# Layer 1 of a two-layer graph network: the turned weights with the key tile innermost, 128 queries in one set of TensorE weights

## The chip, the core and the metric

The kernel runs on one core of a Trainium2 chip. The time is device microseconds of that core for one execution of the whole program; lower is better. TensorE multiplies matrices (PE in the profile, and PEld for its loads of weights), VectorE (DVE), ScalarE (ACT) and GpSimd (POOL) do the rest, and SyncE (SP) starts most of the DMA transfers. Engines run side by side and wait for each other through semaphores; each one works through its own instructions in order.

## What is computed

There are 16 graphs of 1024 nodes with 256 features, and an integer matrix `adj` for each graph. Layer 0 is attention with 8 heads of 32, masked by `adj`. Layer 1 is a graph attention without projections. Cut to what matters here:

```
h = relu(layernorm(x));  x = x + attention_0(h, adj)         # 8 heads, mask adj == 0
h = relu(layernorm(x))
e_k    = leaky_relu(einsum('bid,bjd->bij', h * a_k, h), 0.2)   # k = 0..3
scores = where(adj == k + 1, e_k, -9e15)                       # one of the four, by adj
alpha  = softmax(scores)
x      = x + einsum('bij,bjd->bid', alpha, h)                  # the sums of this change
```

`adj` holds only 0 and 1 in these inputs, so layer 1 uses `a_0` alone. A general path, `layer_1_of_kinds`, stands behind a condition and is not run.

## The kernel before, in words

**Tiles.** A graph is cut into 8 tiles of 128 query nodes (NT = 8), so there are 128 tiles in all. The main loop goes over the tiles s of all graphs, and within a tile over the 8 heads h of layer 0. The order of the work on each engine is written out by hand in this loop (under `tc.manual_schedule()`); nothing moves it. Layer 1 of a tile (class `Edges`) runs 9 tiles behind layer 0 (class `Attend`), and the projections of a tile (class `Piece`) run 9 tiles ahead, all of them spread over the heads of the tile that is in work. So 120 tiles of layer 1 lie inside the main loop; the last ones follow it in a loop of their own, the tail, which lays layer 1 of the remaining tiles behind each other (`last` is true for eight of them; they use other buffers and do the leaky ReLU on VectorE).

**Layer 0 in a tile.** For each head TensorE forms the scores (L461) in one of two PSUM buffers, `sides` (heads 4 and 6 in side 1, the others in side 0, but for the first tiles). VectorE adds the mask and takes the maximum (L473), and in reading the scores it also sets the buffer free. ACT takes the exponential (L490). Then the 128x1024 matrix has to be turned, so that the keys lie on the partitions. Some heads are turned on TensorE (`turn_half`, L590, with the copy L591 on ACT or VectorE), some by blocks: VectorE transposes 32x32 blocks (`blocks_of`, L381), and four DMA transfers put the blocks into their partitions (`placed`, L386). Which heads go by which way depends on the tile: 0, 1, 4 and 5 by blocks, but only 4 and 5 in the first tile of a graph and only 0 and 1 in the last. The keys stand in another order for the heads that usually go by blocks, so where such a head is turned on TensorE its exponential writes in a changed order (L482 to L488): heads 0 and 1 in the first tile of a graph, 4 and 5 in the last. The sums over the values follow (`combine`, L526): four heads of 32 columns beside each other in four column groups of TensorE's array, group 0 at head 7, group 1 at head 3 of the next tile.

**Layer 1 in a tile.** The edge matrix is symmetric, so half of its scores are transposed copies of blocks that are kept in `mirror` (L627), the others are matmuls (L633, at heads 0 and 2). VectorE masks (L656, head 3), ACT and GpSimd bend (L665, L674 to L676), ACT takes the exponential (L680, head 6). This leaves `sel`, 128 queries x 1024 keys. In the next tile:

- head 0: `turn_blocks` (L688) transposes `sel` by 32x32 blocks on VectorE, through the same line L381 as for the heads. `place_blocks` (L691) issues the four transfers into `pT1`.
- heads 5 and 6: `gather` (L694) forms the sums, in two halves of four key tiles each. The weights are the turned matrix, the moved operand is `h1s`, 128 keys x 256 features. The output has 128 queries, in four column groups of 32: for each key tile j and each group a one matmul with 32 columns of weights (L698).
- head 6: `store` divides by the softmax's total and adds the nodes (L705, L707) and writes out (L708).

The layout of the turned matrix before is `[block row b][key tile j][query q]` in each partition, with 8 key tiles of 32 queries each: the 32 queries of one block are contiguous. `placed` moves chunks of 1 KB, 256 elements, and after it one partition holds four groups a of `[j][q]`.

Rows of a tile are loaded in a mixed order and written back in it (`mixed`), so that the order of the queries in the turned matrix is that of the partitions of the sums.

Around the change, the order at the start of a tile is on VectorE: L473 of head 0, the turning of `sel` (L381), L473 of head 1. On TensorE: scores of head 0 (L461), transposes (L590), edge scores, scores of head 1, transposes, L565, projections (L267), scores of head 2.

Of the kernel before, what the change touches and what calls it, by code (L numbers as in the profile page):

```python
# [8 lines left out]
F32 = mybir.dt.float32  # L9
# [8 lines left out]
P = 128  # L18
HEADS = 8
HD = 32  # L20
# [27 lines left out]
def gnn_kernel(  # L48
# [18 lines left out]
    nc = tc.nc  # L67
    B, N, D = x.shape
    NT = N // P
# [3 lines left out]
    NB = P // HD  # L73
# [10 lines left out]
    work = ctx.enter_context(tc.tile_pool(name="work", bufs=2))  # L84
# [294 lines left out]
    def blocks_of(p):  # L379
        blocks = work.tile([P, NB, NT, HD], F32, tag="blocks", bufs=3)  # L380
        nc.vector.transpose(blocks.rearrange("p b j q -> p j b q"), p)  # L381
        return blocks.rearrange("p b j q -> p b (j q)")

    def placed(blocks, pT):
        for a in range(NB):
            nc.sync.dma_start(  # L386
                out=pT[:, a * NT * HD : (a + 1) * NT * HD], in_=blocks[a * HD : (a + 1) * HD]
            )
        return pT.rearrange("p (a j q) -> p j a q", a=NB, j=NT)


    h1s, x1ds, masks = {}, {}, {}
# [22 lines left out]
    class Attend:  # L415
# [82 lines left out]
        def turn_blocks(self, h):  # L498
            self.blocks = blocks_of(self.probs[h][0])

        def place_blocks(self, h):
            self.turned[h] = placed(self.blocks, ptp.tile([P, N], F32, tag="pT", name="pT"))
# [91 lines left out]
    class Edges:  # L594
# [91 lines left out]
            nc.gpsimd.dma_start(out=self.x1, in_=x1ds[self.b][self.rows, :])  # L686

        def turn_blocks(self):  # L688
            self.blocks = blocks_of(self.sel)

        def place_blocks(self):  # L691
            self.pT = placed(self.blocks, self.buffer("pT1", [P, N]))

        def gather(self, half):  # L694

            for j in range(half * NT // 2, (half + 1) * NT // 2):
                for a in range(NB):
                    nc.tensor.matmul(  # L698
                        self.sums[a * HD : (a + 1) * HD, :], lhsT=self.pT[:, j, a], rhs=h1s[self.b][:, j, :],
                        start=(j == 0), stop=(j == NT - 1),  # L700
                    )

        def store(self):
            rec = small.tile([P, 1], F32, tag="rec1")
# [82 lines left out]
    with tc.manual_schedule():  # L787
# [51 lines left out]
        for s in range(B * NT + 1):  # L839
            b, t = divmod(s, NT)  # L840
# [224 lines left out]
```

## Time and profile before

| | us |
|---|---|
| median of 3 runs | 3076.24 |
| lowest and highest | 3071.88, 3076.31 |
| the profiled execution, its own time | 3076.4 |
| its span, first to last instruction | 3074.5 |
| busy: ACT | 2654.5 (86%) |
| busy: GpSimd | 2177.6 (71%) |
| mean granted TensorE clock | 0.996 |

The groups of the profile that belong to the changed steps or lie next to them:

| group | count | busy us | mean ns |
|---|---|---|---|
| L526, sums of layer 0, four column groups | 16384 | 533.4 | 275 |
| L381, turning of `sel` | 120 | 148.8 | 1240 |
| L541, projection of the output, 128 columns of weights, 256 moved | 512 | 131.8 | 380 |
| L707, division and sum | 124 | 60.0 | 484 |

A row of the groups gives line, engine, operation, output and inputs by the names of the program, the shape and the number of instructions; behind the bar the busy time of all of them in us and the mean time of one in ns; then the idle time of the engine just ahead of them and what ended it. On TensorE an fp32 matmul leaves two records, and records overlap: a mean of 380 ns does not say that the next one has to wait so long. Busy is the time that the records cover together.

A row of the order in time gives the start in us from the span's first instruction, the time from the first start to the last end of a run of like instructions, the engine, the line, the names and the shape, the count, and in brackets the idle time ahead of it with what ended it.

### The profile page before, as it was taken

Reading aid. Unit: us, or ns where it says so; the run is one execution under the profiler, and the core shown is the slowest. Engines: PE = TensorE matmul, PEld = TensorE weight load, DVE = VectorE, ACT = ScalarE, POOL = GpSimd, SP = SyncE. Lnnn points to the kernel's source line nnn. Section 1 sums busy time; section 2 is a strip of 40 time slices with the busy share of each in tenths; the row PEclk is TensorE's granted clock in tenths of the full one; section 3 lists DMA queues with packets and bytes.
Section 4 is the critical chain, followed back from the end, with each engine's and each line's share of the span. In section 5 each row is a group of like instructions: output and inputs, shape, how many; then the busy total and the mean of one; then the engine's idle time right before and its main releaser. Section 6 shows DMA issues by size and latency. Waiting matters only on the chain. (4 is left out here: it accounts for less than half of the span.)

```text
span 3074.5 us, 96254 instructions
## 1 busy us (share of the span) xinstructions
PE 2965.6 (96%) x36722; PEld 2230.1 (73%) x36722; DVE 2515.6 (82%) x4453; ACT 2654.5 (86%) x5159; POOL 2177.6 (71%) x2999
## 2 busy tenths in 40 slices
PE   7889999999999999999999999999999999999998
PEld 5667777777777777777777777777777777776664
DVE  5878888888888888888888788888888888888885
ACT  5888888899898998889889888988989888898882
POOL 3657777777777777777777777777777777776542
PEclk9999999999999999999999999999999999999999
DMA  7766777877777786777777777787777777777653
GB/s 245 219 219 205 237 235 222 255 216 243 231 225 243 230 257 209 232 247 220 246 230 228 235 232 243 221 255 221 220 247 228 251 211 235 237 227 236 191 168 100
DMA packets 597828, 695.68 MB, mean 226 GB/s; under 512 B 63280, under 2 KB 528560, under 8 KB 597360
## 3 DMA queue, kind: packets, MB, share of 16 engines
q1 hardware_dynamic: 528288, 477.29, 51.9%
q0 software_dynamic: 66960, 210.04, 21.0%
q8 instruction: 295, 4.83, 0.7%
q10 hardware_dynamic: 2112, 2.10, 0.2%
q14 instruction: 173, 1.42, 0.1%
HBM read 252.98 MB, written 134.22 MB: 126 GB/s over the span
## 5 line engine op out<-in xcount | busy, mean ns | idle before, releaser
L473 DVE CUSTOM_DVE_ANT_0 p<-s,neg 128x1024 f32<-128x1024 f32 x1024 | 1236.2, 1208 | 220.7 <-PE s L461 185.1
L490 ACT ACTIVATE p<-p,nmx 128x1024 f32<-128x1024 f32 x1024 | 1249.4, 1224 | 132.5 <-DVE nmx L473 123.9
L461 PE MATMUL s<-k,qt 128*128 128x512 f32 x2048 | 760.6, 453 | 15.5 <-DVE nmx L473 4.3
L591 ACT COPY pT<-trp 128x512 f32<-128x512 f32 x1024 | 549.4, 590 | 95.3 <-PE trp L590 94.9
L590 PE MATMUL trp<-ident,p 128*128 128x128 f32 x4608 | 604.5, 274 | 4.7 <-ACT pT L591 1.5
L590 PEld LDWEIGHTS trp<-ident,p 128*128 128x128 f32 x4608 | 531.0, 140 | 104.0 <-ACT pT L591 10.8
L381 DVE STREAM_TRANSPOSE blocks<-p 128x1024 f32<-128x1024 f32 x456 | 564.5, 1238 | 12.3 <-ACT p L680 10.6
L526 PE MATMUL acc<-pT,v 128*32 128x128 f32 x16384 | 533.4, 275 | 41.8 <-ACT recT L520 30.0
L526 PEld LDWEIGHTS acc<-pT,v 128*32 128x32 f32 x16384 | 453.5, 110 | 153.0 <-ACT recT L520 85.0
L698 PE MATMUL acc<-h,pT 128*32 128x256 f32 x8192 | 496.9, 382 | 2.8 <-DVE h L707 1.7
L441 POOL TENSOR_SCALAR neg<-adj 128x1024 bf16<-128x1024 int32 x128 | 467.9, 3655 | 42.9 <-ACT neg L453 33.7
L461 PEld LDWEIGHTS s<-k,qt 128*128 128x128 f32 x2048 | 322.9, 191 | 106.3 <-issue 43.0
L698 PEld LDWEIGHTS acc<-h,pT 128*32 128x32 f32 x8192 | 241.8, 109 | 207.8 <-issue 65.6
L676 POOL TENSOR_TENSOR sel<-sel,less 128x1024 f32<-128x1024 f32 x120 | 286.8, 2390 | 68.9 <-ACT less L665 47.6
L633 PE MATMUL s<-h1T,ha 128*128 128x512 f32 (+2 forms) x744 | 272.8, 490 | 2.7 <-ACT h1T L569 1.6
L674 POOL TENSOR_SCALAR less<-top 128x1 f32<-128x1 f32 x120 | 31.9, 266 | 274.0 <-DVE top L656 273.9
L324 POOL DMA_DIRECT2D qd<-halves x240 | 177.5, 780 | 58.7 <-POOL halves L314 31.8
L490 ACT ACTIVATION_READ_ACCUMULATOR p<-p,nmx 128x1 f32 x1024 | 206.8, 202 | 0.0
L510 POOL COPY wide<-rec 128x256 f32<-128x256 f32 x128 | 53.8, 420 | 204.2 <-DVE rec L508 204.2
L330 POOL DMA_DIRECT2D kd<-halves x240 | 172.2, 766 | 35.5 <-POOL halves L314 35.4
L314 POOL TENSOR_TENSOR halves<-full,halves 128x256 fp32r<-128x256 f32 x240 | 176.8, 737 | 20.6
L633 PEld LDWEIGHTS s<-h1T,ha 128*128 128x128 f32 x744 | 126.7, 190 | 70.7 <-issue 45.0
(117 smaller groups left out, 4328.4 us busy)
## 6 DMA issues: line engine op xcount, KB each, us to landing
pT<-blocks SPq DMA_DIRECT2D x2304, 128.0 KB, 3.5
qt<-qd SPq DMA_DIRECT2D x128, 512.0 KB, 4.5
k<-kd SPq DMA_DIRECT2D x128, 512.0 KB, 7.3
adj<-in_adj POOLq DMA_DIRECT2D x127, 512.0 KB, 5.0
qd<-halves POOLq DMA_DIRECT2D x240, 256.0 KB, 2.7
kd<-halves POOLq DMA_DIRECT2D x240, 128.0 KB, 4.1
xb<-in_x POOLq DMA_DIRECT2D x128, 128.0 KB, 4.2
x1d<-x SPq DMA_DIRECT2D x128, 128.0 KB, 4.0
```

The lines of the kernel that those rows point to most:

```text
L324: nc.gpsimd.dma_start(out=qds[self.b][self.first, oc].rearrange("p u w n -> p u (w n)"), in_=halves.unsqueeze(1).to_broadcast([P, 2, 2 * P]),)
L381: nc.vector.transpose(blocks.rearrange("p b j q -> p j b q"), p)
L441: nc.gpsimd.tensor_scalar(self.neg, self.adj, 0.0, MASKED, ALU.is_equal, ALU.mult)
L461: nc.tensor.matmul(self.ps[:, cols], lhsT=self.qt[:, h, :], rhs=keysets[self.b][h][:, cols], start=True, stop=True,)
L473: nc.vector.tensor_tensor_reduce(out=p, in0=sides[h in self.second], in1=self.neg, scale=-SCALE, scalar=FLOOR, op0=ALU.add, op1=ALU.min, a ...
L490: nc.scalar.activation(to, of, AF.Exp, bias=nmx, scale=-1.0, accum_out=self.sums[:, h : h + 1])
L526: nc.tensor.matmul(sums_place[r * HD : (r + 1) * HD, g * P : (g + 1) * P], lhsT=vs[self.b][:, j, place_of(h) : place_of(h) + HD], rhs=self ...
L590: nc.tensor.transpose(tr[:, j, :], p[:, jj * P : (jj + 1) * P], ident)
L591: copy(pT[:, half * 4 : half * 4 + 4, :], tr)
L633: nc.tensor.matmul(self.side[:, cols], lhsT=self.ha[:, c, :], rhs=h1T[:, c, cols], start=(c == 0), stop=(c == NC - 1),)
L676: nc.gpsimd.tensor_tensor(self.sel, self.sel, self.less, ALU.subtract)
L698: nc.tensor.matmul(self.sums[a * HD : (a + 1) * HD, :], lhsT=self.pT[:, j, a], rhs=h1s[self.b][:, j, :], start=(j == 0), stop=(j == NT - 1),)
```

## The change

The edge matrix is no longer turned by the common helper `blocks_of`. `turn_blocks` of `Edges` has its own transpose, which writes each 32x32 block so that the key tile j is innermost: the layout becomes `[block row b][query q][key tile j]`. Neighbouring queries are then 8 elements (32 bytes) apart in a partition; before they were neighbours. The input is read as before.

The four transfers of `placed` are the same: 256 contiguous elements for each group, whatever order they have. After them a partition holds `[a][q][j]`, and since a and q are next to each other, the 128 queries of all four groups for one key tile are one row of elements at a stride of 8. `gather` takes them as one set of 128 columns of weights: for each key tile one matmul with an output of 128 partitions, in place of four with 32. In a tile that is 8 matmuls for 32. The moved operand, the number of key tiles, the place in PSUM (`sums`) and the halves stay. The order of all other instructions on each engine stays too, and the turning of layer 0's heads still goes through `blocks_of`.

```diff
         def turn_blocks(self):
-            self.blocks = blocks_of(self.sel)
+            blocks = work.tile([P, NB, HD, NT], F32, tag="blocks", bufs=3)
+            nc.vector.transpose(blocks.rearrange("p b q j -> p j b q"), self.sel)
+            self.blocks = blocks.rearrange("p b q j -> p b (q j)")
 
         def place_blocks(self):
-            self.pT = placed(self.blocks, self.buffer("pT1", [P, N]))
+            pT = self.buffer("pT1", [P, N])
+            placed(self.blocks, pT)
+            self.pT = pT.rearrange("p (aq j) -> p j aq", j=NT)
 
         def gather(self, half):
 
             for j in range(half * NT // 2, (half + 1) * NT // 2):
-                for a in range(NB):
-                    nc.tensor.matmul(
-                        self.sums[a * HD : (a + 1) * HD, :], lhsT=self.pT[:, j, a], rhs=h1s[self.b][:, j, :],
-                        start=(j == 0), stop=(j == NT - 1),
-                    )
+                nc.tensor.matmul(
+                    self.sums, lhsT=self.pT[:, j], rhs=h1s[self.b][:, j, :],
+                    start=(j == 0), stop=(j == NT - 1),
+                )
```

## The prediction

> **What bounds the kernel now.** I read the shares of the engines first, then the groups by line, then the instructions in order of time of one tile out of the middle (tile 5 of a graph, 1618 to 1633 us), because a mean over 3 ms does not say which wait ends last.
>
> ```profile
> PE 2965.6 (96%) x36722; PEld 2230.1 (73%) x36722; DVE 2515.6 (82%) x4453; ACT 2654.5 (86%) x5159; POOL 2177.6 (71%) x2999
> ...
> L381 DVE STREAM_TRANSPOSE blocks<-p 128x1024 f32<-128x1024 f32 x456 | 564.5, 1238 | 12.3 <-ACT p L680 10.6
> ...
> L698 PE MATMUL acc<-h,pT 128*32 128x256 f32 x8192 | 496.9, 382 | 2.8 <-DVE h L707 1.7
> ```
>
> TensorE is busy 96% of the span, no other engine over 86%. L698, the sums that change, takes 496.9 us: 64 records a tile (each fp32 matmul leaves two). Now the order on TensorE (columns: start, time to the last end, count):
>
> ```profile
> 1618.99 1.04 PE L590 MATMUL trp<-ident,p 128*128 128x128 f32 x8
> 1619.95 1.93 PE L698 MATMUL acc<-h,pT 128*32 128x256 f32 x32
> 1621.82 0.44 PE L237 MATMUL acc<-ident,h 128*128 128x128 f32 x2
> 1622.01 0.71 PE L461 MATMUL s<-k,qt 128*128 128x512 f32 x2
> 1622.65 1.93 PE L698 MATMUL acc<-h,pT 128*32 128x256 f32 x32
> 1624.52 1.16 PE L267 MATMUL acc<-hT,wkT 128*128 128x128 f32 x8
> 1625.43 0.70 PE L461 MATMUL s<-k,qt 128*128 128x512 f32 x2
> ...
> 1630.10 0.73 PE L461 MATMUL s<-k,qt 128*128 128x512 f32 x2
> 1630.66 1.03 PE L590 MATMUL trp<-ident,p 128*128 128x128 f32 x8
> 1631.54 0.38 PE L565 MATMUL acc<-ident,h 128*128 128x128 f32 x2
> 1631.75 1.06 PE L267 MATMUL acc<-hTm,wqT 128*128 128x128 f32 x8
> 1632.57 0.71 PE L461 MATMUL s<-k,qt 128*128 128x512 f32 x2
> ```
>
> Here the start-to-start times are to be read: one group follows the other without a hole, so a group costs what lies between its start and the next. And VectorE in the same stretch:
>
> ```profile
> 1628.81 1.23 DVE L473 CUSTOM_DVE_ANT_0 p<-s,neg 128x1024 f32<-128x1024 f32 x1 [0.18 <-POOL shift L172]
> 1629.96 0.08 DVE L473 DVE_READ_ACCUMULATOR2_ANT nmx<- 128x1 f32 x1
> 1629.96 1.24 DVE L381 STREAM_TRANSPOSE blocks<-sel 128x1024 f32<-128x1024 f32 x1
> 1631.12 1.19 DVE L473 CUSTOM_DVE_ANT_0 p<-s,neg 128x1024 f32<-128x1024 f32 x1
> 1632.24 0.08 DVE L473 DVE_READ_ACCUMULATOR2_ANT nmx<- 128x1 f32 x1
> ```
>
> Heads 0 to 3 share one scores buffer (side 0), so the scores of head 2 (TensorE, 1632.57) cannot start before VectorE's L473 of head 1 has read it (ends 1632.32). That L473 stands right behind the turning of the edge matrix (1629.96), which the change touches. TensorE starts 0.06 us after VectorE's end where it does wait (1630.04 to 1630.10, head 1), so at head 2 the slack is 0.25 - 0.06 = 0.19 us. The kernel is bound by TensorE, but at heads 0 to 2 VectorE is only 0.2 us from the path.
>
> **The change, part by part.**
>
> *The sums.* 32 matmuls a tile of 32 columns of weights become 8 of 128 columns: 64 records become 16, in two halves of 8 records. Four column groups run side by side, so a half takes 1621.82 - 1619.95 = 1.87 us, the second too (1624.52 - 1622.65). The eight full-width records of L267 with 128 columns moved take 1632.57 - 1631.75 = 0.82 us and the eight transposes 0.88, so about 0.107 us for 128 columns moved and 0.215 us for 256: a half will take 8 x 0.215 = 1.72 us. That saves 0.15 us a half, 0.30 a tile. Going over between full width and column groups costs too: eight transposes take 0.96 us ahead of L698 and 0.88 ahead of L565 (0.08); the scores 0.64 ahead of L698 and 0.56 ahead of L590 (0.08); L267 takes 0.91 behind L698 and 0.82 otherwise (0.09). Together **0.55 us a tile** that TensorE no longer needs.
>
> *The weights, now at a stride of 8 elements.* No row shows TensorE loading weights at a stride. 8 loads of 128 columns follow each other in the 0.82 us of L267, 0.10 us each, beside matmuls that are as short. From now on they lie beside matmuls of 0.215 us. A price of up to double is hidden; whatever is over it falls on TensorE 16 times a tile. Lower bound nothing. The nearest row of a strided access in SBUF is an ACT write:
>
> ```profile
> 1514.23 2.18 ACT L490 ACTIVATE p<-p,nmx 128x1024 f32<-128x1024 f32 x1
> ...
> 1517.47 2.22 ACT L490 ACTIVATE p<-p,nmx 128x1024 f32<-128x1024 f32 x1
> ...
> 1519.51 1.16 ACT L490 ACTIVATE p<-p,nmx 128x1024 f32<-128x1024 f32 x1
> ```
>
> These are the exponentials of heads 0, 1 and 2 of a first tile. By L482 to L488 heads 0 and 1 there write at a stride of 4 elements (16 bytes) and the others in order: 2.20 us against 1.15, 1.05 us more for 1024 elements, 1.03 ns each. For 128 columns that is 0.13 us on top of 0.107, 0.24 us against the matmul's 0.215: 0.025 x 16 = 0.4 us a tile. I take nothing, because a price that merely doubles is covered, and keep 0.4 for the range.
>
> *The turning on VectorE.* The 32x32 transpose now writes its elements 32 bytes apart, 128 times. Reading PSUM at a stride is free here (L242 692 ns at a stride against L591 684 ns in order), which is the lower bound, nothing; but this is a write into SBUF, and there the nearest row is the exponential above. By its 1.05 us more, 1.24 becomes 2.29; doubling the part that grows with the elements (1.24 less 0.16, the time of the 128x1 reciprocal L705) gives **1.08 us more**; by the ratio 2.20/1.15 it is 1.13. No row shows an access that a stride makes cheaper. I take 1.08.
>
> The Trainium skill (SBUF — State Buffer, section "SBUF: two separate sides") says that SBUF has lines of 16 bytes, that each access to a new line pays, and that fp32 can be strided by 4 for free. The exponentials are at exactly 4 and pay, so the measurement decides on that figure; the rule itself speaks against both edits, since at 8 elements each write and each weight is in a line of its own. By its free stride alone the sum would not change, by its penalty it is the one above, without a size.
>
> *What lies on the path.* TensorE comes 0.55 us earlier to the next tile's head 0; VectorE follows, since its 0.64 us of waiting for L698 ahead of L707 goes. Then the turning ends 1.08 us later, and with it L473 of head 1, and the scores of head 2 wait. Queued behind them on TensorE are the edge scores L633, the values L344 and all of heads 3 and on, so the wait is a shift of the whole tile. Per tile: 1.08 - 0.19 - 0.55 = **+0.34 us** in tiles 4 to 7. In tile 3 the slack is larger (the same two rows there are 659.43 and 659.91, 0.48, less 0.06 = 0.42): +0.11. In tiles 2 and 1 VectorE also stands idle for 0.26 and 0.57 us between the turning and L473, waiting for scores that are late behind L633: -0.15 and -0.46. In tile 0 TensorE waits for ACT, which has the two slow exponentials, ahead of L526 (0.69 us at 1521.08), and that wait swallows either sign: 0. Sum for a graph: 4 x 0.34 + 0.11 - 0.15 - 0.46 = 0.86 us; for the 120 turnings inside the main loop (15 graphs) +13 us.
>
> *The tail.* After the main loop eight last tiles run through one chain on VectorE and ACT: at 3035.88 L381, then L705, L707, L656, L671, ACT's exponential, and L381 again at 3041.64 (it waits 1.31 us for that exponential). The turning is on it: 8 x 1.08 = +8.6 us; TensorE's shorter sums gain only at the last (-0.3).
>
> *What moves but costs nothing.* The four transfers to pT leave 1.08 us later; the sums that need them start 12.4 us after the turning (1629.96 to 1642.39) and a transfer lands in 3.5 us. Their chunks stay 1 KB. Behind them in SP's queue stand the next queries and keys, needed a tile later; TensorE's waits for these two are 3.9 us in all today.
>
> **Sum.** The profiled execution took 3076.4 us (span 3074.5, 1.9 outside it), the median is 3076.24, so no correction: 3076.4 + 13 + 8 = **3098 us**.
>
> **The rivals.**
> - *The strided write is free* (d = 0), the other sign. Then TensorE's 0.55 us is gain wherever TensorE is the bound; in tile 0, and in tile 7 with its two slow exponentials beside the sums, ACT takes it. 6 x 0.55 x 15 = 50 us: **3027 us**. For it: strided reads of PSUM are free, and no VectorE write at a stride is in the trace. Against it: the exponentials. It decides from d below 0.9 us on, where main loop and tail together come to about nothing.
> - *The strided weights show through* at 0.24 us a load: the gain shrinks to 0.15. Tiles 4 to 7 lose 0.74 each, tile 3 0.51, tile 2 0.25, tile 1 about 0: 3.7 x 15 = 56, with the tail **3140 us**. For it: the same slow row. Against it: it is a write of another engine, and a load has twice the time it needs.
> - *Much dearer accesses* (three times or more for either): over 3200 us; nothing in the trace speaks for it.
>
> That the change does not do what it says is excluded by the instruction order: 2 x 4 matmuls of 128x256 stand where 2 x 16 of 32x256 stood, and nothing else moves.
>
> **How the numbers follow.** The forecast, 3085 to 3115, has 0.45; the free write 0.25; weights that show 0.20; a price of about 0.9 us, which comes to no change, 0.05; much dearer 0.05. The range takes in the free write and the weights at 0.24 us: 3022 to 3150. About 0.2% can be told from no change. Faster: 0.25 and a little of the price near 0.9, 0.27; same 0.10, from that price and the lower edge of the forecast; slower 0.63.
>
> **What would show it.** Right: L698's group at about 2048 records and 16 x 0.215 = 3.4 us a tile; the turning of sel at 2.2 to 2.4 us while that of p stays at 1.24; a new wait of the scores L461 on VectorE's nmx of 0.5 to 1 us a tile. Wrong: the turning of sel still at 1.24 (then the gain stays), or starts of the sums over 0.23 us apart (then the weights show).

## The result, and the profile after

| | before | after |
|---|---|---|
| median, us | 3075.32 | 3106.47 |
| lowest and highest, us | 3071.88, 3076.31 | 3096.22, 3108.1 |
| the profiled execution: time, span, us | 3076.4, 3074.5 | 3096.22, 3094.3 |

The ratio of after to before is 1.0096, with a 95% interval of 1.0073 to 1.012: slower by 31 us. 3098 was forecast.

The profiled execution is the fastest of the four after the change, so it can't be held against the one before as it stands. The first instruction that differs is the first turning of `sel`; it starts at 261.9 us before and at 252.5 us after. Up to there both programs do the same, but the granted TensorE clock is 0.96 before and 0.99 to 1.00 after in these first 260 us (1.00 in both from there on). So 9.4 us of the difference are the start's, and by these two executions the change costs 19.8 + 9.4 = 29 us. The other three executions after, which took 3106 to 3108 us, left no trace; their granted clock was 0.994 to 0.995 for 0.998 in the profiled one, which would fit a slower start, but is not shown to be one. In the main loop (from the first turning to the last L536, 2735.5 us before and 2757.2 after) that is 21.7 us, in the tail behind it 7.6 (77.1 and 84.7).

Two groups of before, and then the groups of after that answer to those shown of before (busy us, mean ns of one, idle time ahead):

```profile
L461 PE MATMUL s<-k,qt 128*128 128x512 f32 x2048 | 760.6, 453 | 15.5 <-DVE nmx L473 4.3
...
L698 PEld LDWEIGHTS acc<-h,pT 128*32 128x32 f32 x8192 | 241.8, 109 | 207.8 <-issue 65.6
```

```profile
PE 2958.2 (96%) x30578; PEld 2496.9 (81%) x30578; DVE 2614.4 (84%) x4453; ACT 2659.5 (86%) x5159; POOL 2175.6 (70%) x2999
...
L461 PE MATMUL s<-k,qt 128*128 128x512 f32 x2048 | 762.4, 453 | 48.6 <-DVE nmx L473 37.5
...
L381 DVE STREAM_TRANSPOSE blocks<-p 128x1024 f32<-128x1024 f32 x448 | 554.7, 1238 | 1.1 <-DMA pT<-blocks 0.5
L701 PE MATMUL acc<-h,pT 128*128 128x256 f32 x2048 | 542.0, 409 | 8.7 <-DMA pT<-blocks 5.6
L701 PEld LDWEIGHTS acc<-h,pT 128*128 128x128 f32 x2048 | 509.7, 333 | 17.9 <-issue 6.7
...
L690 DVE STREAM_TRANSPOSE blocks<-sel 128x1024 f32<-128x1024 f32 x120 | 255.0, 2125 | 0.0
```

The sums have a quarter of the records and are busy longer, 542.0 us for 496.9. The cause stands in the next row: one load of 128 columns takes 333 ns, while loads of this shape in order take 190 ns for the scores L461 and 140 ns for the transposes L590. The turning of `sel` takes 2125 ns for 1240, the turning of the heads is unchanged. And the scores wait for VectorE: 37.5 us on the matmuls, 4.3 before.

The same stretch of tile 5 in order of time, first TensorE, then VectorE (start, time to the last end):

```profile
1620.17 1.03 PE L590 MATMUL trp<-ident,p 128*128 128x128 f32 x8
1621.04 2.17 PE L701 MATMUL acc<-h,pT 128*128 128x256 f32 x8
1623.04 0.38 PE L237 MATMUL acc<-ident,h 128*128 128x128 f32 x2
1623.18 0.72 PE L461 MATMUL s<-k,qt 128*128 128x512 f32 x2
1623.73 2.06 PE L701 MATMUL acc<-h,pT 128*128 128x256 f32 x8
1625.63 1.05 PE L267 MATMUL acc<-hT,wkT 128*128 128x128 f32 x8
1626.44 0.71 PE L461 MATMUL s<-k,qt 128*128 128x512 f32 x2
...
1632.78 1.06 PE L267 MATMUL acc<-hTm,wqT 128*128 128x128 f32 x8
1634.23 0.73 PE L461 MATMUL s<-k,qt 128*128 128x512 f32 x2 [0.39 <-DVE nmx L473]
```

```profile
1630.98 2.13 DVE L690 STREAM_TRANSPOSE blocks<-sel 128x1024 f32<-128x1024 f32 x1
1632.95 1.22 DVE L473 CUSTOM_DVE_ANT_0 p<-s,neg 128x1024 f32<-128x1024 f32 x1
1634.09 0.09 DVE L473 DVE_READ_ACCUMULATOR2_ANT nmx<- 128x1 f32 x1
```

Two things are to be seen. The halves of the sums take 2.00 and 1.90 us from their start to the next group's, more than the 1.87 of each before; from L590 to the scores behind L267 it is 6.27 us for 6.44, a gain of 0.17. So the halves themselves cost 0.16 us more than in column groups, and the gain comes from the groups ahead of and behind them alone, which take 0.33 us less. And the scores of head 2 now start 0.05 us behind VectorE's L473 (1634.18 to 1634.23), with TensorE idle ahead of them: L267, which used to be followed by them after 0.82 us, is now followed after 1.45.

### The profile page after: what moved, and what is told of

It reads as the page before. It is cut to its first block, busy times and chain, and to the rows that moved or that the text cites. A ratio compares the mean times of both kernels' runs of the same rounds, so it can differ in the third digit from the quotient of the medians.

```text
span 3094.3 us, 84215 instructions
## 1 busy us (share of the span) xinstructions
PE 2958.2 (96%) x30578; PEld 2496.9 (81%) x30578; DVE 2614.4 (84%) x4453; ACT 2659.5 (86%) x5159; POOL 2175.6 (70%) x2999
## 3 DMA queue, kind: packets, MB, share of 16 engines
q1 hardware_dynamic: 528288, 477.29, 51.3%
## 5 line engine op out<-in xcount | busy, mean ns | idle before, releaser
L473 DVE CUSTOM_DVE_ANT_0 p<-s,neg 128x1024 f32<-128x1024 f32 x1024 | 1237.4, 1209 | 156.8 <-PE s L461 136.3
L461 PE MATMUL s<-k,qt 128*128 128x512 f32 x2048 | 762.4, 453 | 48.6 <-DVE nmx L473 37.5
L590 PEld LDWEIGHTS trp<-ident,p 128*128 128x128 f32 x4608 | 533.4, 140 | 95.1 <-DVE pT L591 9.6
L590 PE MATMUL trp<-ident,p 128*128 128x128 f32 x4608 | 602.1, 273 | 5.1 <-ACT pT L591 2.1
L526 PEld LDWEIGHTS acc<-pT,v 128*32 128x32 f32 x16384 | 451.4, 110 | 137.7 <-ACT recT L520 80.0
L526 PE MATMUL acc<-pT,v 128*32 128x128 f32 x16384 | 529.2, 274 | 29.3 <-ACT recT L520 25.0
L381 DVE STREAM_TRANSPOSE blocks<-p 128x1024 f32<-128x1024 f32 x448 | 554.7, 1238 | 1.1 <-DMA pT<-blocks 0.5
L701 PE MATMUL acc<-h,pT 128*128 128x256 f32 x2048 | 542.0, 409 | 8.7 <-DMA pT<-blocks 5.6
L701 PEld LDWEIGHTS acc<-h,pT 128*128 128x128 f32 x2048 | 509.7, 333 | 17.9 <-issue 6.7
L461 PEld LDWEIGHTS s<-k,qt 128*128 128x128 f32 x2048 | 322.7, 190 | 148.5 <-DVE nmx L473 80.8
L690 DVE STREAM_TRANSPOSE blocks<-sel 128x1024 f32<-128x1024 f32 x120 | 255.0, 2125 | 0.0
L324 POOL DMA_DIRECT2D qd<-halves x240 | 177.1, 778 | 58.7 <-POOL halves L314 31.8
```

What stands on the lines that cost most here:

```text
L461: nc.tensor.matmul(self.ps[:, cols], lhsT=self.qt[:, h, :], rhs=keysets[self.b][h][:, cols], start=True, stop=True,)
L473: nc.vector.tensor_tensor_reduce(out=p, in0=sides[h in self.second], in1=self.neg, scale=-SCALE, scalar=FLOOR, op0=ALU.add, op1=ALU.min, a ...
L526: nc.tensor.matmul(sums_place[r * HD : (r + 1) * HD, g * P : (g + 1) * P], lhsT=vs[self.b][:, j, place_of(h) : place_of(h) + HD], rhs=self ...
L590: nc.tensor.transpose(tr[:, j, :], p[:, jj * P : (jj + 1) * P], ident)
L690: nc.vector.transpose(blocks.rearrange("p b q j -> p j b q"), self.sel)
L701: nc.tensor.matmul(self.sums, lhsT=self.pT[:, j], rhs=h1s[self.b][:, j, :], start=(j == 0), stop=(j == NT - 1),)
```

## The experiments

They take the two strided accesses apart, put TensorE's gain by itself, and then look for a layout that keeps the gain. Times in the table: ratio to the kernel before, run beside it on the same chip, and from the profile the period from the turning of `sel` in tile 5 of a graph to that in tile 6 (graph at about 1600 us). The four kernels from "write alone" to "write and order" mix up the order of the queries: they time the work and can't stand in for the kernel.

| kernel | ratio (95% interval) | period, us | turning, ns | load, ns |
|---|---|---|---|---|
| before | 1 | 22.46 | 1240 | 109 (32 columns) |
| the change | 1.0096 (1.0073 to 1.012) | 22.96 | 2125 | 333 |
| write alone | 1.016 (1.0146 to 1.0174) | 23.14 | 2125 | 110 (32 columns) |
| weights alone | 0.9986 (0.9976 to 0.9995) | 22.28 | 1240 | 333 |
| weights in order | 0.9837 (0.9821 to 0.9852) | 22.00 | 1240 | 190 |
| write and order | 0.9928 (0.9913 to 0.9942) | 22.49 | 2119 | 191 |
| stride 4 | 1.0055 (1.0041 to 1.007) | 22.81 | 2097 | 325 |
| stride 2 | 0.9857 (0.9842 to 0.9872) | 21.84 | 1243 | 196 |
| pieces of 128 bytes | 0.9845 (0.983 to 0.9861) | 21.80 | 1240 | 190 |

One such period can be off by some tenths. The medians of the same period over the 15 graphs are, row by row, 22.46, 22.95, 23.12, 22.29, 21.85, 22.48, 22.83, 21.91 and 21.89 us.

**The strided write alone.** The edit, against the change:

```diff
-            placed(self.blocks, pT)
-            self.pT = pT.rearrange("p (aq j) -> p j aq", j=NT)
+            self.pT = placed(self.blocks, pT)
...
-                nc.tensor.matmul(
-                    self.sums, lhsT=self.pT[:, j], rhs=h1s[self.b][:, j, :],
+                for a in range(NB):
+                    nc.tensor.matmul(
+                        self.sums[a * HD : (a + 1) * HD, :], lhsT=self.pT[:, j, a], rhs=h1s[self.b][:, j, :],
```

> Only the strided write of the turning is kept; the sums are those of before, in column groups with 32 neighbouring columns of weights, and so read the turned matrix in the wrong order (the output is wrong, the work is the same). Theory (the turning ends 0.89 us later and the scores of head 2 wait for it): TensorE gains nothing, so 0.89 - 0.19 = 0.70 us are lost in tiles 4 to 7, 0.47 in tile 3, 0.21 in tile 2, nothing in tiles 1 and 0; 3.5 us a graph, 52 in 15 graphs, and 7 in the tail: ratio to before 1.019. Rival (the loss comes from the weights, VectorE has room): only the tail is longer, 1.002.

Measured: 1.016, 49 us at a median of 3070, where 59 were expected and the rival had 7. The period grows by 0.68 us (0.70 expected), and the scores wait for VectorE as in the change:

```profile
L461 PE MATMUL s<-k,qt 128*128 128x512 f32 x2048 | 761.7, 453 | 50.2 <-DVE nmx L473 37.4
```

VectorE has no room for the longer turning; beside sums in column groups the write is a loss larger than that of the whole change.

**The strided weights alone.** The edit, against the change:

```diff
-            blocks = work.tile([P, NB, HD, NT], F32, tag="blocks", bufs=3)
-            nc.vector.transpose(blocks.rearrange("p b q j -> p j b q"), self.sel)
-            self.blocks = blocks.rearrange("p b q j -> p b (q j)")
+            self.blocks = blocks_of(self.sel)
```

> Only the sums are changed: 128 columns of weights at a stride of 8 elements, while the turning writes as before (the sums read the wrong order, the work is the same). Theory: loads of 0.33 us still show, but leave TensorE 0.17 us a tile of gain, and without the late turning nothing takes it: 0.17 x 6 x 15 = 15 us, ratio 0.995. Rival (the weights are the loss): 1.005 or more.

Measured: 0.9986, 4 us faster, not the 15 of the theory, and outside the rival. The period is shorter by 0.18 us, as expected. The two profiled executions show more than the medians: from the first turning to the last L536 it is 2722.7 us for 2735.5 before, 12.8 us less and near the 15, and the tail is 1.8 us longer (78.9 and 77.1). But the profiled execution before took 3076.4 us where the 15 executions run beside this kernel have a median of 3070.0, and the one with these weights 3062.9 where its own eleven have 3065.9. How much of the 15 us is kept, between the 4 of the medians and the 12.8 of the traces, stays open.

**Full width with neighbouring columns.** The edit, against before:

```diff
-            self.pT = placed(self.blocks, self.buffer("pT1", [P, N]))
+            self.pT = self.buffer("pT1", [P, N])
+            placed(self.blocks, self.pT)
...
-                for a in range(NB):
-                    nc.tensor.matmul(
-                        self.sums[a * HD : (a + 1) * HD, :], lhsT=self.pT[:, j, a], rhs=h1s[self.b][:, j, :],
+                nc.tensor.matmul(
+                    self.sums, lhsT=self.pT[:, j * P : (j + 1) * P], rhs=h1s[self.b][:, j, :],
```

> The turning of before, and sums with 128 neighbouring columns of weights, 8 matmuls a tile (they read blocks of the wrong queries, the work is the same). Theory (column groups cost TensorE 0.55 us a tile, and the rest of the gain was lost to the strided loads): 0.55 x 6 x 15 = 50 us, ratio 0.984; starts of the sums 0.215 us apart, loads at 0.19 us. Rival (the column groups cost nothing that TensorE would not wait for elsewhere): 1.000.

Measured: 0.9837, 51 us faster; 50 were expected. The halves on TensorE, and the groups that follow them, in the order of time of this kernel:

```profile
1611.01 1.04 PE L590 MATMUL trp<-ident,p 128*128 128x128 f32 x8
1611.88 1.89 PE L698 MATMUL acc<-h,pT 128*128 128x256 f32 x8
1613.61 0.38 PE L237 MATMUL acc<-ident,h 128*128 128x128 f32 x2
1613.74 0.70 PE L461 MATMUL s<-k,qt 128*128 128x512 f32 x2
1614.29 1.89 PE L698 MATMUL acc<-h,pT 128*128 128x256 f32 x8
1616.01 1.05 PE L267 MATMUL acc<-hT,wkT 128*128 128x128 f32 x8
1616.82 0.70 PE L461 MATMUL s<-k,qt 128*128 128x512 f32 x2
```

Its loads of weights, as a group:

```profile
L698 PEld LDWEIGHTS acc<-h,pT 128*128 128x128 f32 x2048 | 379.9, 190 | 60.4 <-issue 3.8
```

A half takes 1.73 and 1.72 us, and the ways in and out are short: from L590 to the scores behind L267 it is 5.81 us for 6.44 before. So 0.63 us is what the column groups cost (0.55 was forecast), and the stride of the weights takes 0.46 of it away again.

That 51 us meets 50 so well is in part luck. The account gave 0.55 us to the tiles 1 to 6 of a graph and nothing to the tiles 0 and 7. By the turnings of `sel` in the two traces, mean of the graphs, the period from one tile to the next is shorter by 0.63 and 0.70 us in tiles 1 and 2, by 0.17 to 0.60 us in tiles 3 to 6 (0.36 in the mean), by 0.60 us in tile 0 and by 0.14 in tile 7: 52.6 us over the main loop. The wait for ACT in tile 0, which was to swallow the gain, did not.

**Late turning, but weights in order.** The write of the change with the sums of the last experiment (`lhsT=self.pT[:, j * P : (j + 1) * P]`).

> The strided write of the turning together with sums that take 128 neighbouring columns of weights (they read blocks of the wrong queries, the work is the same): the late turning without the strided loads. Theory (both are terms on TensorE's path and add up): tiles 4 to 7 lose 0.89 - 0.19 - 0.55 = 0.15 us each, tile 3 gains 0.08, tile 2 0.34, tile 1 0.55; 0.4 us a graph gained, 5 in all, and the tail gives back 7: ratio 1.000. Rival (VectorE's chain sets the pace of the tile, and what TensorE saves is spent waiting at head 2): 1.010 or more.

Measured: 0.9928, 22 us faster. The rival falls: what TensorE saves is not spent at head 2. But the theory's number is missed too, by 0.7%. In tile 5 the period is 22.49 us, 0.03 over before where 0.15 was expected, and in the mean of the graphs the tiles 4 to 7 together lose nothing; in the tiles that gain, the theory gave too little: 0.65 us for 0.34 in tile 2, and 0.57 for nothing in tile 0. So the gain was reckoned too small there, and the loss by the late turning too large in tiles 4 to 7. The write alone shows the latter too: 0.43 to 0.54 us a tile in the mean of the graphs for 0.70 (49 us in all for 59).

**A smaller stride.** The turned matrix is cut into parts of two (or four) key tiles, so that only these are innermost. A part of one block row is then a piece of 256 (512) bytes in the transfers, and the 128 queries stand at a stride of 2 (4) elements:

```diff
-            blocks = work.tile([P, NB, HD, NT], F32, tag="blocks", bufs=3)
-            nc.vector.transpose(blocks.rearrange("p b q j -> p j b q"), self.sel)
-            self.blocks = blocks.rearrange("p b q j -> p b (q j)")
+            JL = 2
+            blocks = work.tile([P, NB, NT // JL, HD, JL], F32, tag="blocks", bufs=3)
+            nc.vector.transpose(blocks.rearrange("p b u q j -> p u j b q"), self.sel)
+            self.blocks = blocks.rearrange("p b u q j -> p b u (q j)")
...
-            placed(self.blocks, pT)
-            self.pT = pT.rearrange("p (aq j) -> p j aq", j=NT)
+            JL = 2
+            parts = pT.rearrange("p (u a x) -> p u a x", a=NB, u=NT // JL)
+            for a in range(NB):
+                nc.sync.dma_start(out=parts[:, :, a], in_=self.blocks[a * HD : (a + 1) * HD])
+            self.pT = pT.rearrange("p (u aq j) -> p u j aq", u=NT // JL, j=JL)
...
-                    self.sums, lhsT=self.pT[:, j], rhs=h1s[self.b][:, j, :],
+                    self.sums, lhsT=self.pT[:, j // 2, j % 2], rhs=h1s[self.b][:, j, :],
```

> The right sums with a layout of four parts, each with two key tiles innermost: the turning writes and the weights are read at a stride of 2 elements (8 bytes), and the transfers move pieces of 256 bytes in place of 1 KB. Theory (an access pays where each element is in another line of 16 bytes): turning at 1.24 us, loads at 0.19 us, starts of the sums 0.215 us apart, ratio as with weights in order, 0.984, if the smaller pieces still land in the 12 us that they have. Rival (every stride pays): turning over 2 us, ratio 1.005 to 1.012.

> The right sums with two parts of four key tiles innermost: write and weights at a stride of 4 elements (16 bytes), pieces of 512 bytes. Theory (each element in another line of 16 bytes pays, as the exponentials at this stride do): turning near 2.1 us, loads near 0.33 us, ratio as the change, 1.010. Rival (a stride of 4 fp32 is still free, as the Trainium skill has it in SBUF — State Buffer): turning 1.24 us, loads 0.19 us, ratio 0.985.

Measured: stride 2 runs at 0.9857 (0.984 expected; its tail is 79.4 us for 76.2 with weights in order), stride 4 at 1.0055, less than the 1.010 expected. The main loop of stride 4 takes 2746.0 us where the change takes 2757.2; its turning is 28 ns and its load 8 ns shorter, and whether that is all is not shown. Their groups (stride 2 first):

```profile
L705 PEld LDWEIGHTS acc<-h,pT 128*128 128x128 f32 x2048 | 392.5, 196 | 53.0 <-issue 9.2 <-DVE h L714 2.9
...
L691 DVE STREAM_TRANSPOSE blocks<-sel 128x1024 f32<-128x1024 f32 x120 | 149.2, 1243 | 0.0
```

```profile
L705 PEld LDWEIGHTS acc<-h,pT 128*128 128x128 f32 x2048 | 499.1, 325 | 21.4 <-issue 10.2 <-DVE h L714 4.1
...
L691 DVE STREAM_TRANSPOSE blocks<-sel 128x1024 f32<-128x1024 f32 x120 | 251.6, 2097 | 0.0
```

At 8 bytes both accesses cost what they cost in order (1243 and 196 ns), at 16 bytes nearly what they cost at 32 (2097 for 2125, 325 for 333). The step lies between a stride of 2 and of 4 fp32 elements. The Trainium skill (SBUF — State Buffer, section "SBUF: two separate sides") has lines of 16 bytes, of which two hits in a row are needed for full speed; that fits both rows. That a stride of 4 fp32 elements would still be free, as it says there too, these runs contradict, for VectorE's write and for TensorE's load. A limit at any spacing from 8 to just under 16 bytes would fit the rows as well; a stride of 3 was not run.

**No stride, smaller pieces.** The layout before the change, but the four transfers put 128 queries of a key tile next to each other, in pieces of 128 bytes:

```diff
-            self.pT = placed(self.blocks, self.buffer("pT1", [P, N]))
+            pT = self.buffer("pT1", [P, N])
+            self.pT = pT.rearrange("p (j a q) -> p j a q", a=NB, j=NT)
+            for a in range(NB):
+                nc.sync.dma_start(
+                    out=self.pT[:, :, a],
+                    in_=self.blocks[a * HD : (a + 1) * HD].rearrange("p b (j q) -> p b j q", q=HD),
+                )
+            self.pT = pT.rearrange("p (j aq) -> p j aq", j=NT)
...
-                for a in range(NB):
-                    nc.tensor.matmul(
-                        self.sums[a * HD : (a + 1) * HD, :], lhsT=self.pT[:, j, a], rhs=h1s[self.b][:, j, :],
+                nc.tensor.matmul(
+                    self.sums, lhsT=self.pT[:, j], rhs=h1s[self.b][:, j, :],
```

> The right sums with no stride at all: the turning of before, 128 neighbouring columns of weights, and transfers in pieces of 128 bytes that put them there. Theory (the transfers have 12 us in the main loop, only the tail waits for them; there stride 2 with four times the pieces took 3.2 us more than the weights in order): main loop as with weights in order, tail 7 us longer than there, ratio 0.986. Rival (eight times the pieces of these transfers crowd the DMA engines): waits of the sums L526 and of the new sums for pT, ratio 0.99 or more.

Measured: 0.9845 (0.986 expected), so the rival falls. The page of this kernel shows what the pieces cost the DMA engines:

```profile
DMA packets 1056533, 694.91 MB, mean 230 GB/s; under 512 B 587568, under 2 KB 987312, under 8 KB 1056112
...
q1 hardware_dynamic: 987040, 477.29, 59.0%
```

With weights in order, at 528288 packets, this queue took 52.8%. The 6 points more cost the main loop nothing here: it takes 2681.0 us for 2683.7 with weights in order. The sums L526 wait for pT 20.1 us in all, 23.7 with weights in order and 11.4 before; the scores L461 wait 7.6 us for their keys, 2.5 with weights in order. The tail is 79.9 us for 76.2 with weights in order, 3.7 us more where 7 were expected.

Stride 2 and the pieces of 128 bytes give the right sums and both beat the kernel before, by 1.4 and 1.5%, and so the change; their intervals overlap, so these runs do not tell which is better.

## Why the number was right, and which steps were not

The time lies in the range, and the sign and the rough split (main loop +21.7 for +13, tail +7.6 for +8) came out. The sum did not come out for the reasons given: two terms were wrong in opposite directions, and that they partly cancel is luck. By tiles, mean of the graphs: +0.32 to +0.43 us in tiles 4 to 7 for +0.34, +0.32 in tile 3 for +0.11, -0.14 in tile 2 for -0.15, -0.15 in tile 1 for -0.46, and -0.10 in tile 0 for 0.

1. **TensorE's gain by full width, 0.55 us a tile: right, a little small.** With neighbouring columns a half takes 1.73 us for the 1.72 forecast, and the whole stretch 0.63 us less. The kernel gains 51 us for the 50 of the first rival's account, but not in the tiles that this account named: tile 0 gains too, tiles 3 to 6 less. VectorE's wait for the sums ahead of the division, which was to go, shrinks there from 81.3 to 58.7 us in all, and in the change it stays (83.2).
2. **"I take nothing" for the strided weights: this step failed.** A load of 333 ns for 190 is more than the matmul hides: the eight records of the second half take 2.06 us from the first start to the last end, so starts are (2.06 - 0.38)/7 = 0.24 us apart, and 0.22 with weights in order ((1.89 - 0.38)/7). That is 2.3 times the 0.10 us of L267's loads, more than the double that was held to be covered, and it is the price that the rival had from ACT's exponentials. The gain left is 0.17 us for the 0.15 which the rival gave it.
3. **The turning, +1.08 us: mis-sized.** It is 2125 - 1240 = 885 ns more. It lies below the 1.05 to 1.13 that were worked out of ACT's row and of doubling; the row was the right one for the kind, not for the size.
4. **The slack of 0.19 us ahead of head 2, and the shift of all that follows: right.** Write alone moves the period by 0.68 us, 0.885 less 0.19 being 0.70, and in the change both terms add up: 0.68 - 0.18 = 0.50, and the period is 22.96 for 22.46.
5. **The forecast for tiles 4 to 7, +0.34 us: the sum of 2 and 3.** 0.38 us of lost gain less 0.19 us of cheaper turning make +0.53 of it; measured +0.50 in tile 5.
6. **The tail, 8 x 1.08: right in its path, mis-sized with step 3.** Nine turnings lie behind the last L536; they take 2.03 us there for 1.25 before, 7.1 us in all, and the tail is 7.6 us longer.

How much hangs on step 2 the experiment with late turning and weights in order shows: that is the forecast's own case with the true price of the write, and it is faster than before, 0.9928. With the write priced rightly and the weights at nothing, the forecast's sum would have come to about no change (1.000), not to a loss. Beside full-width sums the strided weights cost more than the strided write: 46 us (0.9837 to 0.9986) to 52 us (0.9928 to 1.0096) against 28 us (0.9837 to 0.9928) to 34 us (0.9986 to 1.0096); the 49 us of the write alone are those beside column groups, where TensorE gains nothing that could take up a part of the wait. It takes both strides to turn the 51 us of gain into a loss.

The first rival (the write is free) is refuted by the 2125 ns. The second (weights that show) was right in its mechanism; its 3140 was too high, about half of it because it carried the same 1.08 (with 0.885 its sum gives about 3122), most of the rest because the tiles 4 to 7 lose less than it adds up.

## What to carry to other kernels

A stride in SBUF that looks free in the access pattern can be paid by the engine that writes it and again by the one that reads it. Here 8 bytes between fp32 elements cost next to nothing (1243 ns for 1240, 196 for 190), while 16 and 32 bytes made a VectorE write and a TensorE load take 1.7 to 1.8 times as long, and 16 bytes an ACT write 1.9 times. When a load of weights is said to be hidden, its slow price has to be compared with the matmul beside it, not its price in order: 0.24 us and more beside 0.215 was enough to lose about 70% of the gain (0.17 us is left of 0.63). And where wider weights need another layout, it can come from the transfers (smaller pieces) as well as from a strided write, if these have time; here they had 12 us, and pieces of an eighth of the size cost 3.7 us in the tail and nothing that was seen in the main loop's time.

## What was not expected

The price of a strided element is nearly the same on two engines: a load of 128 columns every 0.24 us is 1.9 ns a column, and VectorE's turning, 2125 ns less the 156 of a 128x1 instruction, is 1.9 ns an element. In order the two differ little as well (0.82 us for 8 loads of 128 columns are 0.8 ns, 1240 less 156 ns are 1.06 ns), so "double" is only a rough rule for these two; 1.9 ns an element fits both better. ACT's exponentials, 2.2 us for 1024 elements as a whole, come near to it. Whether one place in SBUF sets it is not shown.

Column groups cost more than their matmuls: the four groups run side by side nearly at the pace of one, but the four ways from full width into groups and back took 0.06 to 0.10 us each (L590 0.96 us for 0.87, L461 0.64 for 0.55, L237 0.19 for 0.13, L267 0.91 for 0.81), and each half came out 0.14 to 0.15 us longer (1.87 for 1.73 and 1.72). Together that is the 0.63 us a tile behind the 1.6% that the full-width sums gain.
